# A graph layer on one core: messages turned by the scaled W_o1, 48 tiles prepared alone, fetches a chunk ahead, 36 blocks summed after the last message

## The chip, the core and the metric

The kernel runs on one core of a Trainium2 chip. The core has five engines with queues of their own: PE (matrix products; its weight loads are listed as PEld), DVE or VectorE, ACT or ScalarE, POOL or GpSimd, and SP, which only issues transfers. Sixteen DMA engines serve all queues. The metric is the device time of one execution in microseconds (us); the time before is the median of three runs.

## The reference, cut to what matters

There are 12500 nodes with 128 features, and 400000 edges with 20 features each. `dst` is sorted, `src` is not; messages are gathered by `dst` and summed by `src`.

```python
def smu(x, alpha=0.01, mu=2.5):
    return ((1 + alpha) * x + (1 - alpha) * x * erf(mu * (1 - alpha) * x)) / 2

hx = maximum(layernorm(x), 0.0)
h = hx @ W_in2f.T
Wij = smu(f_ij @ W_f1.T + b_f1) @ W_f2.T + b_f2
Wij = Wij * rcut_ij[:, None]
x_ij = h[dst] * Wij
agg = segment_sum(x_ij, src, num_segments=12500)
out = x + smu(agg @ W_o1.T + b_o1) @ W_o2.T + b_o2
```

`smu` is a Gelu plus a small linear part; the kernel computes it as `Gelu(ZS * v) + LIN * v` and puts the remaining factor into the next matrix.

## The kernel before, in words

**Units of work.** A tile is 128 edges (3125 of them), a group 4 tiles (782), a super 8 tiles (two groups). A bin is 128 nodes (98 of them, the last with 84). The edges are worked in 9 passes (`PARTS`: 59, 59, 59, 59, 48, 37, 27, 27 and 16 supers). In a pass every message is written to a buffer in HBM, ordered by its source bin, with 129 numbers per row (128 values and its row in the bin). While the next pass prepares its messages, the buffer of the pass before is read back and summed into `agg`, in "blocks": one block is 128 rows of one bin, summed with a one-hot matrix in one product. A bin of pass k has Q[k] blocks (6 in the first four passes, then 5, 4, 3, 3, 2). A fetch brings 12 row-columns at most, so 4 bins of 3 blocks in the last pass but one; there are four such row buffers (`rw`), and `AHEAD = 4`.

**A group.** PE multiplies the edge features (L551, `hide`), ACT takes the Gelu (L559), DVE adds the linear part (L567, `smooth`), PE multiplies by W_f2 (L604, `weigh`). For the gather, h in three bf16 parts lies in HBM; SP loads the 42 rows that a group's sorted targets can reach (L451, at a row number read from `base_i`), DVE makes a one-hot matrix from the targets (L460), and PE multiplies (L585). ACT copies that out of PSUM (L593, `take`), DVE multiplies the two (L614, `mix`), PE transposes the four tiles (L624, `turn`), and ACT scales each by its edge weight into the message tile `ms` (L634, `send`). DVE puts the row in the bin beside it (L631), and POOL writes one tile at a time with an indirect transfer (L637). Where it writes is counted in between: a running count per bin on DVE (L485, `bins`), products that rank the tile's edges (L499 to L502, `count`), a maximum (L529, `read`) and the address (L538, `number`).

**The order.** PE, DVE, ACT and SP run in the order in which the program is written; POOL's instructions are placed by a planner, by readiness. In the loop over groups an iteration writes: `turn(g)`, `send(g)`, `step()`, `number`, `weigh`, `gather`, `take` for g+1, half of the blocks due (`parts`), `mix(g+1)`, `step()`, `hide`, `bend`, `count`, `smooth` for g+2, `bins(g+3)`, `read(g+2)`, the other half of the blocks, `step()`. So DVE's small cast of group g stands in its queue behind the work of the iteration before.

**The opening.** Tiles 0 to 23 (`FEW`) have their targets in the first 128 rows of h, which are computed first and kept on the chip (`h_first`); their gather is three products (L583) and needs no window. Meanwhile 14 opening steps (rows 128 to 511 of h, targets and bins of the first chunk of 512 tiles) are taken two per `step()`. Later steps of pass 0 (the other six chunks of indices: `head_of`, whose `fetched` issues the index loads and whose `based` is the first to use them; statistics and rows of h) are spread over the rest of that pass.

**The end.** After the last group, the last pass's buffer is fetched and summed. Every four bins form an output unit: a product with W_o1 (L250), a Gelu (L251), the linear part on DVE (L255), four products with W_o2 (L260), the sum with x and bias (L264) and the store. x is loaded four units ahead on ACT's queue (L240), and POOL adds the bias to it (L246). Each x tile is asked for when the unit four before it has been stored.

## Time and profile before

| what | us |
|---|---|
| three runs: median (lowest to highest) | 4151.15 (4150.53 to 4153.11) |
| the profiled execution: time | 4134.27 |
| its span | 4132.4 |
| first scatter, last scatter (L637 starts) | 19.15, 4023.79 |
| busy: PE, DVE, ACT, POOL | 3500.0, 3498.8, 1854.6, 3048.9 |
| ACT waiting to write a message for a free buffer (L634) | 474.5 |
| DVE waiting for fetched rows (L679), 11 times | 147.2 |
| mean granted PE clock | 0.959 |

A timeline line reads: start (us), duration (us), engine, line of the kernel, operation, written tile <- read tiles, partitions x elements, and in brackets the idle time of that engine before it and what ended it. A group line ends with busy us, mean ns of one, and idle us before. A windows line gives a stretch and its length, then busy us and instruction counts of PE, PEld, DVE, ACT and POOL, and then PE's granted clock, the share of the 16 DMA engines, and GB/s.

### The profile page before, as it was taken

The page shows a single profiled execution, that of the slowest core. Times are in us where ns is not written, and L with a number is a line of the kernel's source. Part 1 is how long each engine was busy: PE and PEld are TensorE (multiplying, and loading weights), DVE is VectorE, ACT ScalarE, POOL GpSimd, SP SyncE. Part 2 cuts the span into 40 slices and gives each one's busy share as a digit, 9 for nine tenths or more (in the row PEclk, how much of TensorE's full clock was granted, in tenths as well). Part 3 has the DMA queues.
Part 4 walks back from the last instruction along what each step waited for, and adds up shares of the span by engine and source line. Part 5 has one row for each costly group of instructions (what it writes and reads, how often), then busy time and mean ns, then how long its engine had stood idle before and what let it go on. Part 6 is the DMA issues. An engine that isn't in the chain of part 4 may idle for free. (4 is left out here: it accounts for less than half of the span.)

```text
span 4132.4 us, 67973 instructions
## 1 busy us (share of the span) xinstructions
PE 3500.0 (85%) x18032; PEld 2218.3 (54%) x18032; DVE 3498.8 (85%) x8551; ACT 1854.6 (45%) x4810; POOL 3048.9 (74%) x3173
## 2 busy tenths in 40 slices
PE   6767886988887888869888879998799889898888
PEld 2334444555554555545555546665466556565567
DVE  6898886988887988869888869998799889898887
ACT  3446553544444444435444434444344444444431
POOL 4777777777777777777777777777777777777772
PEclk8999998999998999989999989999899999999999
DMA  4875665766656766647666647776588689787568
GB/s 144 234 198 174 189 186 176 211 193 193 196 156 200 211 197 190 199 140 214 214 189 194 201 149 209 215 212 199 173 233 230 176 244 248 211 234 219 170 184 240
DMA packets 564967, 820.60 MB, mean 199 GB/s; under 512 B 178779, under 2 KB 379234, under 8 KB 564444
## 3 DMA queue, kind: packets, MB, share of 16 engines
q1 hardware_dynamic: 450650, 602.06, 51.1%
q0 software_dynamic: 100320, 207.40, 15.2%
q10 hardware_dynamic: 13602, 6.73, 0.6%
q8 instruction: 143, 2.34, 0.3%
q14 instruction: 252, 2.06, 0.2%
HBM read 442.51 MB, written 373.37 MB: 197 GB/s over the span
## 5 line engine op out<-in xcount | busy, mean ns | idle before, releaser
L637 POOL DMA_INDIRECT buf<-ms,ix x3125 | 3008.6, 963 | 1006.6 <-issue 424.8
L634 ACT ACTIVATE ms<-pt,w_sb 128x128 f32<-128x128 f32 x3125 | 890.9, 368 | 1442.2 <-PE pt L624 848.6
L692 PEld LDWEIGHTS pg<-se,rw 128*128 128x128 f32 x8036 | 1060.6, 193 | 267.0 <-issue 225.1
L692 PE MATMUL pg<-se,rw 128*128 128x128 f32 x8036 | 1154.2, 281 | 8.5 <-DVE se L679 8.5
L485 DVE SCALAR_TENSOR_TENSOR so<-irow_ps,hi_f,so 128x98 f16<-128x98 f32 x3116 | 989.8, 318 | 82.6
L624 PE MATMUL pt<-ident,mt 128*128 128x128 f32 x3125 | 507.2, 286 | 524.7 <-DVE mt L614 522.0
L604 PE MATMUL pw<-sm,w_f 128*128 128x512 f32 x1564 | 902.9, 660 | 42.6 <-DVE sm L567 40.7
L551 PE MATMUL pu<-f,w_f 128*128 128x512 f32 x1564 | 824.5, 610 | 0.0
L559 ACT ACTIVATE ge<-pu 128x512 f32<-128x512 f32 x782 | 469.1, 600 | 555.4 <-PE pu L551 540.2
L679 DVE TENSOR_TENSOR se<-irow_ps,rw 128x1536 f32<-128x1536 f32 (+1 forms) x345 | 587.8, 1704 | 148.4 <-DMA rw<-buf 147.2
L614 DVE SCALAR_TENSOR_TENSOR mt<-pw,b,hg 128x512 f32<-128x512 f32 x782 | 583.3, 746 | 145.8 <-ACT hg L593 133.9
L624 PEld LDWEIGHTS pt<-ident,mt 128*128 128x128 f32 x3125 | 348.2, 143 | 624.5 <-DVE mt L614 618.2
L567 DVE SCALAR_TENSOR_TENSOR sm<-pu,ge 128x512 f32<-128x512 f32 x782 | 534.9, 684 | 151.6 <-ACT ge L559 147.1
L593 ACT ACTIVATE hg<-ph 128x512 f32<-128x512 f32 x782 | 469.1, 600 | 170.0 <-PE ph L585 99.6
L529 DVE TENSOR_REDUCE sl<-pc 128x4 f32<-128x392 f32 x782 | 434.7, 556 | 0.0
L604 PEld LDWEIGHTS pw<-sm,w_f 128*128 128x128 f32 x1564 | 240.3, 194 | 164.2 <-DVE sm L567 136.4
L585 PE MATMUL ph<-oh,hw 126*128 126x512 bf16 x776 | 306.4, 395 | 0.0
L551 PEld LDWEIGHTS pu<-f,w_f 128*128 128x128 f32 x1564 | 258.7, 199 | 59.5 <-issue 52.0
L499 PE MATMUL pc<-so,tri 128*128 128x392 f16 x782 | 260.6, 333 | 1.9 <-DVE so L485 1.1
L501 PE MATMUL pc<-so,rest_h 128*128 128x294 f16 x781 | 227.4, 291 | 0.0
L501 PEld LDWEIGHTS <-rest_h 128*128 128x128 f16 x781 | 77.1, 99 | 272.4 <-issue 272.3
L460 DVE TENSOR_SCALAR oh<-rbc,prow 128x1024 bf16<-128x1024 bf16 x388 | 192.8, 497 | 1.5 <-DMA rbc<-rel_dram 1.5
(151 smaller groups left out, 1357.5 us busy)
## 6 DMA issues: line engine op xcount, KB each, us to landing
rw<-buf SPq DMA_DIRECT2D x292, 774.0 KB
rbc<-rel_dram SPq DMA_DIRECT2D x389, 256.0 KB
buf<-zero SPq DMA_DIRECT2D x243, 387.0 KB
buf<-ms,ix POOLq DMA_INDIRECT x3125
buf<-zero SPq DMA_DIRECT2D x193, 258.0 KB
rw<-buf SPq DMA_DIRECT2D x49, 645.0 KB
f<-in_f_t SPq DMA_DIRECT2D x390, 80.0 KB
hw<-h_dram SPq DMA_DIRECT2D x776, 31.5 KB
```

What stands on the lines that cost most here:

```text
L485: nc.vector.scalar_tensor_tensor(so[:, j], irow_ps[:, :NB], hi_f[:, t + j:t + j + 1], so[:, j - 1] if j else before, op0=ALU.is_equal, op1 ...
L551: nc.tensor.matmul(pu[:, :n], w_f1, loaded[g // PER][0][:, o:o + n], start=True, stop=True)
L559: nc.scalar.activation(ge[:, :n], units_of[g][:, :n], AF.Gelu, scale=ZS)
L567: nc.vector.scalar_tensor_tensor(sm[:, :n], units_of.pop(g)[:, :n], LIN, hidden[g][:, :n], op0=ALU.mult, op1=ALU.add)
L593: nc.scalar.activation(hg[:, :n], rows_of[g][:, :n], AF.Copy)
L604: nc.tensor.matmul(pw[:, :n], w_f2, hidden.pop(g)[:, :n], start=True, stop=True)
L614: nc.vector.scalar_tensor_tensor(mt[:, :n], pws.pop(g)[:, :n], b2, rows_of.pop(g)[:, :n], op0=ALU.add, op1=ALU.mult)
L624: nc.tensor.transpose(pt[:, j, :], mt[:, j * P:(j + 1) * P], ident)
L634: nc.scalar.activation(ms[:, j, 0:P], pt[:, j], AF.Copy, scale=w_sb[:, t + j:t + j + 1])
L637: i = nc.gpsimd.indirect_dma_start(out=bufs[k][:, :], out_offset=bass.IndirectOffsetOnAxis(ap=ix[:, j:j + 1], axis=0), in_=ms[:, j, :], in ...
L679: nc.vector.tensor_tensor(se[:, :m], irow_ps.unsqueeze(1).to_broadcast([P, m, P]), rows_in[c][:, :m, P:P + 1].to_broadcast([P, m, P]), op= ...
L692: nc.tensor.matmul(pgs[0][:, g, :], rows_in[c][:, o, 0:P], sel[c][:, o, :], start=(q == 0), stop=(q == Q[k] - 1))
```

## The change

It has ten parts, all in one diff. (1) W_o1, scaled by LIN, takes the place of the identity in `turn`, so that a message reaches the buffer already multiplied by W_o1; the sums are then `LIN * agg @ W_o1.T`, and the output units lose their product. Gelu's scale becomes ZS / LIN, and the linear part is a plain sum. (2) In the output units Gelu reads `agg` itself, and the sum is done on POOL (`between`); the four PSUM tiles rotate for W_o2's products. (3) The row-in-bin numbers are copied by ACT instead of DVE. (4) The scaling in the layer norm goes from DVE to ACT, with a new tile `down` for minus mean times the reciprocal. (5) Bin and row in the bin come from float arithmetic (`whole_bins`: rounding by a large constant) instead of an integer shift and mask: five operations in place of four. (6) 48 tiles instead of 24 are prepared with `h_first`. (7) One opening step per `step()` instead of two. (8) `fetched` of chunk c+1 stands ahead of the steps of chunk c. (9) In the last pass 36 of the 294 blocks are left out of the loop and summed after the last group, with the last pass's first fetches written ahead of them. (10) w_o1 is loaded at the start, on ACT's queue, instead of by SP later.

```diff
@@ -34,6 +34,7 @@
 ROW = P + 1
 BIG = 2047.0
 ZP = 128
+ROUND = 12582912.0
 
 
 @with_exitstack
@@ -184,6 +185,7 @@
     x_sb = agg.rearrange("p (b d) -> p b d", d=D)
     mv = const.tile([P, NB, 2], F32, name="mv")
     rstd = const.tile([P, NB], F32, name="rstd")
+    down = const.tile([P, NB], F32, name="down")
 
     def stats(pool, b):
         st = pool.tile([P, 6], F32, name="st")
@@ -193,13 +195,14 @@
     def deviations(a, b):
         nc.scalar.activation(rstd[:, a:b], mv[:, a:b, 1], AF.Sqrt, bias=eps)
         nc.vector.reciprocal(rstd[:, a:b], rstd[:, a:b])
+        nc.vector.scalar_tensor_tensor(down[:, a:b], mv[:, a:b, 0], -1.0, rstd[:, a:b], op0=ALU.mult, op1=ALU.mult)
 
     def rows_of_h(b, n, xn, xt, left, hs, psum):
 
         def normed():
             for j in range(n):
-                nc.vector.tensor_scalar(xn[:, j], x_sb[:, b + j, :], mv[:, b + j, 0:1], rstd[:, b + j:b + j + 1],
-                                        op0=ALU.subtract, op1=ALU.mult)
+                nc.scalar.activation(xn[:, j], x_sb[:, b + j, :], AF.Identity, scale=rstd[:, b + j:b + j + 1],
+                                     bias=down[:, b + j:b + j + 1])
 
         def turned():
             pt = kept[0] = psum("pt")
@@ -248,11 +251,11 @@
     def half(unit, po, ge):
         w = width(unit)
         nc.tensor.matmul(po[:, :w], w_o1, agg[:, unit[0] * P:unit[0] * P + w], start=True, stop=True)
-        nc.scalar.activation(ge[:, :w], po[:, :w], AF.Gelu, scale=ZS, bias=bz)
+        nc.scalar.activation(ge[:, :w], po[:, :w], AF.Gelu, scale=ZS / LIN, bias=bz)
 
     def bent(unit, po, ge, sm):
         w = width(unit)
-        nc.vector.scalar_tensor_tensor(sm[:, :w], po[:, :w], LIN, ge[:, :w], op0=ALU.mult, op1=ALU.add)
+        nc.vector.tensor_add(sm[:, :w], po[:, :w], ge[:, :w])
 
     def rest(unit, sm, py):
         b, n, rows = unit
@@ -286,7 +289,7 @@
         def fill(i, engine):
             engine.memset(fbufs[i], 1.0)
 
-        FEW = 3 * SUP
+        FEW = 6 * SUP
 
         def parts_tile():
             return edge.tile([P, GRP, 3, D], BF, name="hs")
@@ -295,6 +298,13 @@
 
         def bank(name):
             return ps2.tile([P, GRP, P], F32, name="pg")
+
+        def whole_bins(to, sf, si):
+
+            nc.vector.tensor_copy(sf, si)
+            nc.vector.tensor_scalar(to, sf, 1.0 / P, -(P - 1) / (2.0 * P), op0=ALU.mult, op1=ALU.add)
+            nc.vector.tensor_scalar(to, to, ROUND, None, op0=ALU.add)
+            nc.vector.tensor_scalar(to, to, -ROUND, None, op0=ALU.add)
 
         def head_of(c):
 
@@ -303,6 +313,7 @@
             s0, m = a // GRP, (n + GRP - 1) // GRP
             rw = rowp.tile([P, ROWS, ROW], F32, name="rw").rearrange("p q r -> p (q r)")
             di, si, rel = rw[:, 0:n].bitcast(I32), rw[:, CH:CH + n].bitcast(I32), rw[:, 2 * CH:2 * CH + n]
+            sf = rw[:, 0:n]
             rb = parts_tile()[:, :, 0, :]
             z = 0 if c else FEW
             base_f = edge.tile([1, CH // GRP], F32, name="base_f")
@@ -357,12 +368,11 @@
                 nc.vector.tensor_scalar(base_i[:, :early], base_f[:, :early], float(HEAD * P - WIN), None, op0=ALU.min)
 
             def binned():
-                nc.vector.tensor_scalar(di[:, z:], si[:, z:], 7, None, op0=ALU.arith_shift_right)
-                nc.vector.tensor_copy(hi_f[:, a + z:a + n], di[:, z:])
+                whole_bins(hi_f[:, a + z:a + n], sf[:, z:], si[:, z:])
 
             def placed():
-                nc.vector.tensor_scalar(di[:, z:], si[:, z:], P - 1, None, op0=ALU.bitwise_and)
-                nc.vector.tensor_copy(lo_b[:, a + z:a + n], di[:, z:])
+                nc.vector.scalar_tensor_tensor(lo_b[:, a + z:a + n], hi_f[:, a + z:a + n], -float(P), sf[:, z:],
+                                               op0=ALU.mult, op1=ALU.add)
 
             return dict(fetched=fetched, based=based, spread=spread, lowered=lowered, turned=turned, written=written,
                         limits=limits, bounded=bounded, binned=binned, placed=placed)
@@ -372,6 +382,7 @@
         ds = edge.tile([P, FEW], I32, name="ds", bufs=1)
         ss = edge.tile([P, FEW], I32, name="ss", bufs=1)
         dsf = edge.tile([P, FEW], F32, name="dsf", bufs=1)
+        ssf = edge.tile([P, FEW], F32, name="ssf", bufs=1)
         h_first = const.tile([P, 1, 3, D], BF, name="h_first")
         nc.sync.dma_start(ds, dst_col[:, 0:FEW])
         nc.scalar.dma_start(x_sb[:, 0:1, :], bin_rows(x, 0, 1))
@@ -382,6 +393,7 @@
         nc.gpsimd.dma_start(w_f1[0:R, :], w_f1_t)
         nc.gpsimd.dma_start(w_f1[R:R + 1, :], b_f1)
         nc.sync.dma_start(fbufs[0][0:R, :], f_t[:, 0:SUP * P])
+        nc.scalar.dma_start(w_o1, w_o1_t)
         nc.scalar.dma_start(x_sb[:, 1:HEAD, :], bin_rows(x, 1, HEAD - 1))
         nc.gpsimd.dma_start(w_f2, w_f2_t)
         nc.gpsimd.dma_start(b2, b_f2.rearrange("o p -> p o"))
@@ -402,7 +414,6 @@
         def late_loads():
 
             nc.sync.dma_start(w_sb[:, CH:NT], w_col[:, CH:NT])
-            nc.sync.dma_start(w_o1, w_o1_t)
 
         def later_loads():
             nc.sync.dma_start(w_o2, w_o2_t)
@@ -426,7 +437,7 @@
             if s > 0:
                 nc.sync.dma_start(fb[0:R, :n], f_t[:, e0:e0 + n])
             loaded[s] = (fb,)
-            if s > 3:
+            if s > 2:
                 targets(s)
 
         def targets(s):
@@ -621,14 +632,14 @@
             pt = ps1.tile([P, GRP, P], F32, name="pt")
             mt = mixed.pop(g)
             for j in range(n):
-                nc.tensor.transpose(pt[:, j, :], mt[:, j * P:(j + 1) * P], ident)
+                nc.tensor.matmul(pt[:, j, :], mt[:, j * P:(j + 1) * P], w_o1, start=True, stop=True)
             mixed[g] = pt
 
         def send(g):
 
             t, n = groups[g]
             ms = msg.tile([P, GRP, ROW], F32, name="ms")
-            nc.vector.tensor_copy(ms[:, :n, P], lo_b[:, t:t + n])
+            nc.scalar.activation(ms[:, :n, P], lo_b[:, t:t + n], AF.Copy)
             pt = mixed.pop(g)
             for j in range(n):
                 nc.scalar.activation(ms[:, j, 0:P], pt[:, j], AF.Copy, scale=w_sb[:, t + j:t + j + 1])
@@ -717,11 +728,10 @@
                 done += 1
 
         WAIT = 4
+        LEFT = 36
         def few_bins():
-            nc.vector.tensor_scalar(ds, ss, 7, None, op0=ALU.arith_shift_right)
-            nc.vector.tensor_copy(hi_f[:, 0:FEW], ds)
-            nc.vector.tensor_scalar(ds, ss, P - 1, None, op0=ALU.bitwise_and)
-            nc.vector.tensor_copy(lo_b[:, 0:FEW], ds)
+            whole_bins(hi_f[:, 0:FEW], ssf, ss)
+            nc.vector.scalar_tensor_tensor(lo_b[:, 0:FEW], hi_f[:, 0:FEW], -float(P), ssf, op0=ALU.mult, op1=ALU.add)
 
         def other_starts():
             m = tiles_of(0)
@@ -762,6 +772,7 @@
         loaded[0] = (fbufs[0], None, h_first.rearrange("p b k d -> p (b k d)"))
         hide(0)
         nc.vector.tensor_scalar(w_f2, w_f2, GC, None, op0=ALU.mult)
+        nc.vector.tensor_scalar(w_o1, w_o1, LIN, None, op0=ALU.mult)
         for b in range(1, HEAD):
             stats(edge, b)
         deviations(1, HEAD)
@@ -838,12 +849,16 @@
         loads = [lambda a=a, n=n: old_piece(HEAD + a, n) for a, n in chunks(NB - HEAD, PIECE)]
         single = [lambda b=b: stats(edge, b) for b in range(HEAD, NB)]
         steps = [one["placed"], loads.pop(0), one["limits"]]
+        heads_of = [named(lambda c=c: head_of(c),
+                          ("fetched", "based", "spread", "lowered", "turned", "written", "binned", "placed", "limits"))
+                    for c in range(1, NC)]
+        steps.append(heads_of[0].pop(0))
         for c in range(1, NC):
-            mine = named(lambda c=c: head_of(c),
-                         ("fetched", "based", "spread", "lowered", "turned", "written", "binned", "placed", "limits"))
             if loads:
                 steps.append(loads.pop(0))
-            for f in mine:
+            if c + 1 < NC:
+                steps.append(heads_of[c].pop(0))
+            for f in heads_of[c - 1]:
                 steps.append(f)
                 if c > 1:
                     steps.append(single.pop(0))
@@ -863,9 +878,7 @@
 
             nonlocal taken_steps, slot
             if opening:
-                for _ in range(2):
-                    if opening:
-                        opening.pop(0)()
+                opening.pop(0)()
                 return
             slot += 1
             while taken_steps < COUNT and taken_steps * 3 * (eps_of[0][1] * PER - 15) < slot * COUNT:
@@ -877,9 +890,8 @@
             k = epoch[s]
             g0, ng = eps_of[k][0] * PER, min(eps_of[k][1] * PER, NG - eps_of[k][0] * PER)
             i = g - g0
-            if g == 2:
-                assert len(opening) == 2
-                targets(3)
+            if g == (FEW // SUP - 3) * PER:
+                assert not opening
             if g % PER == 0:
                 load(s + 3)
             if i == 0:
@@ -904,8 +916,9 @@
                 choose(k - 1, 0)
             lo = hi = 0
             if k and i >= WAIT:
-                lo = len(work) * (i - WAIT) // (ng - WAIT)
-                hi = len(work) * (i + 1 - WAIT) // (ng - WAIT)
+                upto = len(work) - (LEFT if k == EPOCHS - 1 else 0)
+                lo = upto * (i - WAIT) // (ng - WAIT)
+                hi = upto * (i + 1 - WAIT) // (ng - WAIT)
             if g:
                 turn(g)
                 send(g)
@@ -930,6 +943,7 @@
             assert k == 0 or taken_steps == COUNT
         k = EPOCHS - 1
         begin(k)
+        parts(k - 1, len(work))
         choose(k, order_of[k][0])
 
 
@@ -950,24 +964,26 @@
 
         def other(i, names):
             turns[i] += 1
-            return names[turns[i] % 2]
+            return names[turns[i] % len(names)]
+
+        def part_of(unit):
+            return agg[:, unit[0] * P:unit[0] * P + width(unit)]
 
         def first_half():
             unit = ready.pop(0)
-            po = ps1.tile([P, GRP * P], F32, name=other(0, ("pu", "ph")))
             ge = edge.tile([P, GRP * P], F32, name="ge")
-            half(unit, po, ge)
-            opened.append((unit, po, ge))
+            nc.scalar.activation(ge[:, :width(unit)], part_of(unit), AF.Gelu, scale=ZS / LIN, bias=bz)
+            opened.append((unit, ge))
 
         def between():
-            unit, po, ge = opened.pop(0)
+            unit, ge = opened.pop(0)
             sm = edge.tile([P, GRP * P], F32, name="sm")
-            bent(unit, po, ge, sm)
+            nc.gpsimd.tensor_add(sm[:, :width(unit)], part_of(unit), ge[:, :width(unit)])
             smoothed.append((unit, sm))
 
         def second_half():
             unit, sm = smoothed.pop(0)
-            py = ps1.tile([P, GRP, P], F32, name=other(1, ("pw", "pt")))
+            py = ps1.tile([P, GRP, P], F32, name=other(0, ("pu", "ph", "pw", "pt")))
             rest(unit, sm, py)
             summed.append((unit, py))
 
```

## The prediction

> **What bounds the kernel now.** I read the page first. PE and DVE are both busy 85% of the span, GpSimd 74%, and the chain of waits is spread over twenty lines, so no total names the limit. I then read GpSimd's own timeline in the middle of the run.
>
> ```profile
> PE 3500.0 (85%) x18032; PEld 2218.3 (54%) x18032; DVE 3498.8 (85%) x8551; ACT 1854.6 (45%) x4810; POOL 3048.9 (74%) x3173
> L637 POOL DMA_INDIRECT buf<-ms,ix x3125 | 3008.6, 963 | 1006.6 <-issue 424.8
> ```
> ```profile
> 1012.72 0.96 POOL L637 DMA_INDIRECT buf<-ms,ix  x1 [0.30 <-DMA buf<-ms,ix]
> 1013.99 0.96 POOL L637 DMA_INDIRECT buf<-ms,ix  x1 [0.30 <-issue]
> 1015.25 0.95 POOL L637 DMA_INDIRECT buf<-ms,ix  x1 [0.30 <-ACT ms L634]
> ```
>
> The scatter of one tile takes 0.96 us, and the next one starts 0.30 us later whatever releaser is named: 1.263 us from start to start, 5.05 us for a group of four tiles. 3124 such steps make 3945.6 us. The first scatter starts at 19.15 us and the last at 4023.79, so 4004.6 us lie between them: GpSimd's issue is the bound, and all that can be won there is 59 us of holes. What is left is 19 us ahead and 108.6 us behind. Where are the holes?
>
> ```profile
> 23.06 0.95 POOL L637 DMA_INDIRECT buf<-ms,ix  x1 [0.30 <-issue]
> 31.05 0.95 POOL L637 DMA_INDIRECT buf<-ms,ix  x1 [7.03 <-issue]
> 34.83 0.96 POOL L637 DMA_INDIRECT buf<-ms,ix  x1 [0.30 <-issue]
> 40.91 0.96 POOL L637 DMA_INDIRECT buf<-ms,ix  x1 [5.12 <-ACT ge L559]
> 56.88 0.96 POOL L637 DMA_INDIRECT buf<-ms,ix  x1 [0.30 <-issue]
> 68.78 0.96 POOL L637 DMA_INDIRECT buf<-ms,ix  x1 [10.94 <-issue]
> ```
>
> In the first ten groups, the holes beyond the 1.263 add up to 31.4 us (6.7, 4.8, 2.0, 10.6, 3.1, 2.9, 1.4 ahead of groups 1, 2, 3, 5, 6, 9, 10). Groups 19 to 98 have some 5 us, the last pass (groups 750 to 781) 9 us; the rest are single scatters that are a little slow. The second place is the end, where GpSimd has no scatter left:
>
> ```profile
> 4060.83 1.13 PE L260 MATMUL pw<-w_o,sm 128*128 128x128 f32 x8
> 4061.80 1.02 PE L250 MATMUL ph<-agg,w_o 128*128 128x512 f32 x2
> 4062.66 1.95 PE L692 MATMUL pg<-se,rw 128*128 128x128 f32 x16
> 4064.48 1.13 PE L260 MATMUL pt<-w_o,sm 128*128 128x128 f32 x8
> 4065.44 1.02 PE L250 MATMUL pu<-agg,w_o 128*128 128x512 f32 x2
> ```
> ```profile
> 4030.00:4040.00 10.00, 8.09 (x49) 7.83 (x49) 6.26 (x8) 0.70 (x2) 0.00 (x0) 0.64 0.81 263
> 4040.00:4070.00 30.00, 30.00 (x212) 25.44 (x212) 24.45 (x31) 5.50 (x8) 8.97 (x8) 1.00 0.95 279
> 4070.00:4100.00 30.00, 30.00 (x217) 25.91 (x216) 25.06 (x30) 6.12 (x9) 10.40 (x9) 1.00 0.99 290
> 4100.00:4120.00 20.00, 20.00 (x147) 17.42 (x146) 14.42 (x21) 3.50 (x6) 8.03 (x7) 1.00 0.62 183
> ```
>
> PE runs without a gap at 3.64 us per output unit of four bins: 1.82 for the sums, 0.96 for W_o2, 0.86 for W_o1 (starts to starts). But the last three columns (clock, DMA share, GB/s) say that the 16 DMA engines are 95 to 99% busy as well.
>
> **The change, part by part.**
>
> *Start.* VectorE's chain to the first message gets a reciprocal's follower (0.17, as L195's 0.16) and the scaling of W_o1 (0.22, as L764), the four integer operations become five, and the turn is longer (next part): +0.9 us. L721 stands there with 4.85 us and ends at 8.98, its twin L723 takes 0.18; GpSimd's fills run from 4.61 to 8.94. I take it that the new first arithmetic operation waits for the fills too. The bound on the other side is that the delay belongs to the integer shift and goes with it: -4.7. The Trainium skill (Advanced Engine Details and Errata, Mode Summary under VectorE Performance Modes) says that VectorE's second SBUF port is GpSimd's too, and that two-port instructions and GpSimd block each other; by that the wait stays, and the two ends of the rows agree with it in time.
>
> *Turn.* 3125 transposes (one instruction each, 109 ns start to start) become products with W_o1 (two instructions, 112 ns as L692): 0.44 us per group become 0.90, +0.46 on PE, of which 0.05 to 0.15 hides behind the next product's wait for VectorE (weigh waits for sm). The bound below is nothing, where VectorE sets the pace. It only counts where the groups are prepared more slowly than 5.05 us. I read that pace from the turns' starts after each pass boundary: 4.65 us in passes 1 to 3, 4.82 in pass 5, 5.02 in pass 6, 4.84 in pass 7, 5.43 in the last. PE idles ahead of the turn (the waits, by window) 70.5 us in 115 groups of pass 1, 13.0 us in 61 groups of pass 5 (0.21 each), 12.7 us in 47 groups of pass 6 (0.27). So pass 5 becomes 5.03 at most, still below 5.05; pass 6 some 5.17, 50 groups x 0.12 = 6 us, of which 3 are covered by the lead that messages have after a boundary (4 us). Together **+3**, with ends 0 and +72 (no idle time takes anything: the slower rival).
>
> *The bin numbers of a message go from VectorE to ScalarE.* The trace has no such operation on ScalarE; the 128x1 square root takes 0.28, a 128x128 copy advances by 0.285, VectorE's own cast by 0.11. I take 0.2. ScalarE has 2.34 us of work in 5.05 per group and runs it while PE turns, so it costs nothing; without that cover 0.2 x 782. VectorE gains 0.11 per group. It waits for a free message buffer, as the first copy behind it does already (474.5 us of waits by ScalarE), so nothing new is queued behind it. What counts: group 1's message was done at 28.1, but VectorE's cast stood behind four other operations until 30.1, and the scatter waited for it.
>
> *Opening.* 48 tiles from the first 128 rows, one step per call, 14 calls for 14 steps, the rows' scaling on ScalarE, chunk 1's indices fetched a chunk ahead (the window loads of groups 6 to 11 go from SP, 2.9 us a pair; their gather costs two more matmuls, 0.43). Hole by hole: group 1 loses 2.6 (cast) and 0.85 (three scalings on VectorE), gets 0.45: 6.7 to 3.7. Group 2: PE stood 3.5 us for L330, which now lies two calls ahead of the transposes: 4.8 to 1. Group 3: 2.0 to 0.5. Group 5: VectorE stood 7.57 us for chunk 1's indices.
>
> ```profile
> 59.20 0.26 DVE L317 COPY base_i<-rw 1x128 int32<-1x128 int32 x1 [7.57 <-DMA rw<-in_dst_col]
> ```
>
> Two more steps now lie between fetch and use, about a group or 5 us: 10.6 to 2.5. Group 6: 3.1 to 2. Group 9 (chunk 2's indices, 4.46 us of waiting): 2.9 to 0. Group 10: 1.4 to 0.5. Sum 31.4 to 10: **-21**. Ends: -28 and -8. Later in pass 0 VectorE loses 98 scalings (0.28 each) and gets one more operation per chunk (0.45 x 7): **-2** of the 5 us.
>
> *Last pass.* 36 of 294 blocks leave: over 28 groups 2.6 matmuls each, 0.29 on PE, about 0.24 on VectorE; the turn adds 0.46, the cast takes 0.11. The pace stays at about 5.4, but scatters no longer wait for VectorE's cast (group 780: message done 4016.4, scatter 4018.7): **-3**. The 36 blocks (72 x 0.112 = 8.1 us on PE) fall into the 10.5 us between the last turn (4018.44) and the first selection of the last sums (4028.93), in which PE sat 8.5 us: no cost. Without that cover the rest beyond 10.5 us counts. They hold all four row buffers, so SP's fetches wait for them as well as for the last scatters; only stores stand behind.
>
> *Output.* W_o1 leaves: 0.86 of 3.64 us, PE's bound becomes 2.78. Gelu reads agg; the sum goes to GpSimd (two adds of 1.27, as L246: 2.54 per unit). By PE alone 24 x 0.86 = -21. By the DMA row 0.97 x 3.64 = 3.53 us of transfers per unit: -3. Between them: the shares times their stretches from 4026 on add up to 87 us, so transfers could end at 4113, some 19 us before the end, of which about 5 remain for the last unit's chain: -14 at most. I take **-11**, the clock (0.64 around 4035, since PE sat idle) among it.
>
> Sum: 0.9 - 21 - 2 + 3 - 3 - 11 = **-33 us**. The profiled execution took 4134.27 us (span 4132.4, 1.9 around it), 16.9 below the median of the three runs, 4151.15. I set the difference against the median: **4118 us**.
>
> **Rivals.**
> (a) *Transfers hold the output* at 3.53 or more: -22 in all, 4129. For it: the share of 0.99. Against: it falls to 0.62 while PE still works.
> (b) *GpSimd's queue holds the output.* If the bias add of a later unit, which waits for its rows of x, stands ahead of the sum, a loop closes over two units: x issue to bias 4.9 us (5.79 us idle before one), two adds 2.54, W_o2 1.13, store 0.69 and hops: 9.3 us, 4.65 per unit early, about 4.2 on average: +13 instead of -11, 4142. Against it: over three units, which is the order by readiness, it gives 3.1. The Trainium skill (GPSIMD Engine Reference, Engine selection) advises against adds on GpSimd, some twice VectorE's time; the rows have 1.27 against 0.68.
> (c) *The opening keeps half its holes*, since 14 calls at one step last until group 4 with GpSimd starved: -10 instead of -21, 4129; with the queue (b) together, 4150.
> (d) *PE becomes the bound of the middle, slower.* If the 0.46 adds to every group's pace, it passes 5.05 already in pass 1 (5.11): 3 each in passes 1 to 3, then 5.30 x 92 groups, 5.28 x 70, 5.48 x 50, 5.30 x 50 less 3 us lead each: 9 + 20 + 13 + 18 + 9 = 69, last pass +3. In all +39, 4190. It decides once 0.24 of the 0.46 is not absorbed in pass 5. For it: PE is 95.8% busy from 3000 to 3200. Against: much of that is modelled ends, and the idle times above.
> (e) *No effect*: the opening's waits only move and the output stays: near 4147.
>
> **How the numbers follow.** Forecast 0.53, (a) 0.12, (b) 0.09, (c) 0.09, (d) 0.12, (e) 0.05. The likeliest's own range is 4103 to 4134. Leaving out the upper part of (d) and the best of the forecast gives 4094 to 4156. A measurement tells 0.2% (8.3 us) from no change: below 4142.8 lie nearly all of the forecast, (a), (c), half of (b): 0.76; within, the rest of (b), (e): 0.10; above, (d) and mixtures: 0.14.
>
> **What would show it.** Right: scatters 1.263 us apart from group 12 on, holes of about 10 us ahead of it, L317 waiting under 3 us, output units 3.1 to 3.4 us apart, last scatter near 4002. Wrong: holes all through passes 4 to 7 with PE back to back (d); GpSimd waiting for x with a sum behind it (b); a first scatter at 15 us (the shift's own delay).

## The result, and the profile after

| | before | changed |
|---|---|---|
| median of four runs, us (lowest to highest) | 4150.84 (4149.83 to 4153.11) | 4107.88 (4107.29 to 4114.07) |
| ratio, 95% interval | | 0.9897 (0.9885 to 0.9909) |
| the profiled execution, us | 4134.27 | 4108.47 |
| first scatter, last scatter | 19.15, 4023.79 | 19.90, 4001.50 |
| holes between scatters: groups 0 to 11 | 32.1 | 7.8 |
| groups 12 to 117 (rest of pass 0) | 8.2 | 4.6 |
| passes 1 to 7 | 9.1 | 15.7 |
| last pass | 9.6 | 7.8 |
| from the last scatter to the end of the span | 108.6 | 105.1 |

The changed kernel is 43 us faster by the medians and 25.8 us by the two profiled executions. Holes are counted as in the prediction: the distance between two starts of scatters, less 1.263 us for every scatter. The step that ends at the first scatter of group 12 is counted with groups 0 to 11, and so at each later boundary. Both columns add up: 3945.6 us of steps plus 59.0 of holes before, 36.0 after.

The page of the changed kernel, its first part and the group of the scatters:

```profile
PE 3668.0 (89%) x21117; PEld 2553.0 (62%) x21117; DVE 3445.1 (84%) x7657; ACT 1948.2 (47%) x5690; POOL 3081.7 (75%) x3199
L648 POOL DMA_INDIRECT buf<-ms,ix x3125 | 3011.3, 964 | 981.5 <-issue 384.1
```

PE has gained 168 us of work and 3085 instructions and is busy 89% of the span; the kernel is faster all the same, because GpSimd's idle time ahead of its scatters fell from 1006.6 to 981.5. Its timeline in the opening, the three scatters of the first twelve groups that waited longer than 0.6 us, and that of group 5:

```profile
27.43 0.96 POOL L648 DMA_INDIRECT buf<-ms,ix  x1 [2.67 <-ACT ms L645]
...
47.80 0.96 POOL L648 DMA_INDIRECT buf<-ms,ix  x1 [0.30 <-ACT ms L645]
...
66.23 0.96 POOL L648 DMA_INDIRECT buf<-ms,ix  x1 [3.18 <-ACT ms L645]
...
83.32 0.96 POOL L648 DMA_INDIRECT buf<-ms,ix  x1 [1.75 <-ACT ms L645]
```

Group 5, which had waited 10.94, starts its scatter at 47.80 with the usual 0.30. Three holes of more than a microsecond are left, ahead of groups 1, 8 and 11. The start, on VectorE (first lines) and GpSimd (the fills):

```profile
3.89 5.10 DVE L304 CAST ssf<-ss 128x48 f32<-128x48 int32 x1
9.02 0.19 DVE L305 TENSOR_SCALAR hi_f<-ssf 128x48 f32<-128x48 f32 x1
...
4.61 0.97 POOL L290 MEMSET f<- 128x1024 f32 x1
...
7.97 0.97 POOL L290 MEMSET f<- 128x1024 f32 x1
```

The new first arithmetic operation takes the old one's place: it stands until the last fill is over. At the other end, the last sums:

```profile
3998.39 0.49 PE L635 MATMUL pt<-w_o,mt 128*128 128x128 f32 x2 [0.92 <-DVE mt L625]
3998.72 10.49 PE L703 MATMUL pg<-se,rw 128*128 128x128 f32 x92
4009.58 0.69 DVE L690 TENSOR_TENSOR se<-irow_ps,rw 128x512 f32<-128x512 f32 x1
```

After the last turn PE has 92 instructions, 46 blocks, to do, and VectorE makes the first selection of the last sums only at 4009.58, 8.1 us after the last scatter (a selection is the one-hot matrix of a fetch, L690). Before, it came at 4028.93, 5.1 us after.

### The profile page after: what moved, and what is told of

Same layout as the page of the kernel before. It is cut to its first block, busy times and chain, and to the rows that moved or that the text cites. A ratio compares the mean times of both kernels' runs of the same rounds, so it can differ in the third digit from the quotient of the medians.

```text
span 4106.6 us, 74086 instructions
## 1 busy us (share of the span) xinstructions
PE 3668.0 (89%) x21117; PEld 2553.0 (62%) x21117; DVE 3445.1 (84%) x7657; ACT 1948.2 (47%) x5690; POOL 3081.7 (75%) x3199
## 3 DMA queue, kind: packets, MB, share of 16 engines
q1 hardware_dynamic: 449760, 601.83, 54.7%
q0 software_dynamic: 100320, 207.40, 15.9%
## 4 chain that ended last, share of the span: by engine, by line
PE 38%; DVE 28%; DMA 19%; ACT 6%; issue 5%; POOL 2%; DVEq 0%; SPq 0%; ACTq 0%; POOLq 0%
DMA buf<-ms,ix 17%; PE pt L635 11%; PE pg L703 8%; DVE se L690 8%; PE pw L615 8%; PE pu L562 7%; DVE mt L625 5%; DVE so L496 4%; DVE sm L578 3%; DVE sl L540 3%; ACT ms L645 2%; ACT ge L570 2%; POOL buf L648 2%; PE ph L596 2%; DVE agg L716 1%
## 5 line engine op out<-in xcount | busy, mean ns | idle before, releaser
L648 POOL DMA_INDIRECT buf<-ms,ix x3125 | 3011.3, 964 | 981.5 <-issue 384.1
L635 PE MATMUL pt<-w_o,mt 128*128 128x128 f32 x6250 | 883.7, 285 | 386.0 <-DVE mt L625 382.4
L635 PEld LDWEIGHTS pt<-w_o,mt 128*128 128x128 f32 x6250 | 768.5, 194 | 472.9 <-DVE mt L625 468.9
L615 PE MATMUL pw<-sm,w_f 128*128 128x512 f32 x1564 | 823.0, 609 | 10.7 <-DVE sm L578 8.8
L562 PE MATMUL pu<-f,w_f 128*128 128x512 f32 x1564 | 807.3, 598 | 0.0
L690 DVE TENSOR_TENSOR se<-irow_ps,rw 128x1536 f32<-128x1536 f32 (+1 forms) x345 | 588.0, 1704 | 114.0 <-DMA rw<-buf 109.1
L604 ACT ACTIVATE hg<-ph 128x512 f32<-128x512 f32 x782 | 468.5, 599 | 59.7 <-PE ph L596 42.9
L642 ACT ACTIVATE ms<-lo_b 128x4 f32<-128x4 bf16 x782 | 160.1, 205 | 339.8 <-DMA buf<-ms,ix 339.4
L596 PE MATMUL ph<-oh,hw 126*128 126x512 bf16 x770 | 297.0, 386 | 0.0
```

The lines of the kernel that those rows point to most:

```text
L562: nc.tensor.matmul(pu[:, :n], w_f1, loaded[g // PER][0][:, o:o + n], start=True, stop=True)
L615: nc.tensor.matmul(pw[:, :n], w_f2, hidden.pop(g)[:, :n], start=True, stop=True)
L635: nc.tensor.matmul(pt[:, j, :], mt[:, j * P:(j + 1) * P], w_o1, start=True, stop=True)
L648: i = nc.gpsimd.indirect_dma_start(out=bufs[k][:, :], out_offset=bass.IndirectOffsetOnAxis(ap=ix[:, j:j + 1], axis=0), in_=ms[:, j, :], in ...
L690: nc.vector.tensor_tensor(se[:, :m], irow_ps.unsqueeze(1).to_broadcast([P, m, P]), rows_in[c][:, :m, P:P + 1].to_broadcast([P, m, P]), op= ...
```

## The experiments

The runs were made on four chips, in the groups of the table; the kernel before ran beside each group. On three of these chips every kernel, the unchanged one too, takes about a quarter longer; what they can tell is said with each reading. From the last scatter to the end, kernels with the same code there differ by some 4 us from trace to trace (105.1 to 109.4 on the chips of 4100 us, 103.5 to 107.1 on the others). Columns: median; ratio to the kernel before on the same chip; holes of groups 0 to 11, 12 to 117, passes 1 to 7, last pass; and the tail after the last scatter, all in us.

| kernel | median | ratio (95%) | 0-11 | 12-117 | 1-7 | last | tail |
|---|---|---|---|---|---|---|---|
| before, again (before: 5237.7) | 5229.1 | 1.0012 (0.9976 to 1.0048) | 35.5 | 150.2 | 934.8 | 46.5 | 112.1 |
| turn_plain | 4981.0 | 0.9538 (0.9489 to 0.9586) | 22.2 | 119.3 | 736.8 | 38.4 | 114.8 |
| open_24 | 5031.2 | 0.9646 (0.9599 to 0.9692) | 23.7 | 126.8 | 761.3 | 47.0 | 107.1 |
| left_none | 5021.3 | 0.9618 (0.9571 to 0.9666) | 16.8 | 125.7 | 791.4 | 48.7 | 102.2 |
| changed, again (before: 5268.8) | 5091.4 | 0.9662 (0.9604 to 0.9720) | 16.5 | 134.7 | 815.3 | 49.3 | 103.5 |
| sum_dve | 5084.7 | 0.9642 (0.9586 to 0.9699) | 14.4 | 129.2 | 821.9 | 49.6 | 102.1 |
| fetch_late (before: 4140.6) | 4126.6 | 0.9966 (0.9953 to 0.9978) | 17.8 | 10.4 | 16.7 | 7.2 | 109.4 |
| cast_dve | 4120.2 | 0.9947 (0.9930 to 0.9963) | 13.0 | 7.4 | 18.7 | 9.4 | 106.7 |
| fills_act | 4107.1 | 0.9918 (0.9901 to 0.9934) | 8.4 | 5.0 | 18.0 | 6.6 | 105.4 |
| best_sum | 4102.2 | 0.9910 (0.9893 to 0.9926) | 8.4 | 6.0 | 15.9 | 10.1 | 97.9 |
| turn_plain, again (before: 5273.6) | 5036.1 | 0.9575 (0.9515 to 0.9635) | 14.8 | 125.8 | 754.6 | 54.7 | 115.5 |
| open_24, again | 5097.8 | 0.9676 (0.9617 to 0.9734) | 25.4 | 131.7 | 825.4 | 54.0 | 106.7 |

### The kernel before, once more

> The kernel before, unchanged, with a trace of another execution. Its first traced execution took 4134.3 us, the median of its runs is 4150.8; the changed kernel's traced execution (4108.5) agrees with its median (4107.9). So the two traces differ by 25.8 us and the medians by 43.0, and 17 us of the gain lie where no trace shows them yet. Theory A (the old trace was one lucky execution): a new trace takes about 4150 us and shows the 16 us as more holes between scatters, in the opening or in the passes. Theory B (tracing itself changes this kernel): the new trace takes 4134 again, with 59 us of holes, and the timed runs 4150.

Neither theory was tested: the chip was another one, and the kernel took 5229 us. The timeline of that execution in pass 3, first PE, then ScalarE:

```profile
1995.37 0.38 PE L585 MATMUL ph<-oh,hw 126*128 126x512 bf16 x1
1996.26 1.02 PE L551 MATMUL pu<-f,w_f 128*128 128x512 f32 x2
...
2000.62 0.60 ACT L593 ACTIVATE hg<-ph 128x512 f32<-128x512 f32 x1 [3.83 <-remote]
2006.33 0.60 ACT L559 ACTIVATE ge<-pu 128x512 f32<-128x512 f32 x1 [5.11 <-remote]
```

Single operations last as long as on the first chip (scatter 0.96, copy 0.60, Gelu 0.60). But the copy that reads `ph` starts 4.9 us after that product has ended, and the Gelu that reads `pu` 9.1 us after, and the profile finds no other work that they waited for ("remote" is what it says when it knows no releaser). The semaphore events that the trace has for these two waits come 0.02 and 0.03 us ahead of the starts, so the hand-over itself is late there. The traces of these three chips hold only about a third of the semaphore events of the others (36 thousand here, 95 thousand in the trace of before), so a releaser that they name is worth less. The bound of the middle is no longer GpSimd's issue: holes are spread over all passes, 1.5 us in every group (934.8 in 632).

### The whole change, once more, and the sum on VectorE

```diff
-            nc.gpsimd.tensor_add(sm[:, :width(unit)], part_of(unit), ge[:, :width(unit)])
+            nc.vector.tensor_add(sm[:, :width(unit)], part_of(unit), ge[:, :width(unit)])
```

> The changed kernel, unchanged, beside the kernel before on whatever chip this call gets. In the call before this one every kernel took 20 to 26% longer, with the same durations of single instructions but pauses of 2 to 9 us in which ScalarE starts nothing though its inputs have long been there. If that belongs to that chip: here about 4108, a ratio to before of 0.990, and a trace with 36 us of holes. If it belongs to the kernels' day-to-day spread: above 4900 again, with a ratio near 0.96, as the variants had.

> The changed kernel with the sum of an output unit on VectorE (0.68 us) instead of GpSimd (1.27). In the changed trace PE waits for that sum in 15 of 25 units, 0.3 to 1.8 us each, 13 us in all, and units are 3.30 us apart. If GpSimd's two adds per unit set the pace: units fall to 2.8 to 3.0, time 7 to 12 us less (4096 to 4101). If the transfers set it (share 1.01 of the 16 DMA engines from 4040 to 4080): units stay at 3.2 to 3.3, time within 3 us of the changed kernel (4105 to 4108), and PE waits for the sum as long, since the sum waits for a buffer that a store has to free.

The unchanged change gives 0.966 there, 177 us. The quarter is thus not the kernel's usual spread, since the third chip below is back at 4140; and the change is worth more where hand-overs are late. The tail reads nearly as on the first chip (103.5 against 105.1); the opening's holes are twice as large (16.5 against 7.8). With the sum on VectorE the two ratios cannot be told apart, and the tail is only 1.3 us shorter, less than it differs by between traces. But inside the tail the effect can be seen: from the first product with W_o2 to the last it takes 74.5 us instead of 79.9, and PE waits 8.2 us for the sums instead of 13.2. Neither expectation holds as it stands: units are 3.1 us apart on average instead of 3.3, and PE's wait shrinks. The rest of the tail took the gain back in this execution: the first product comes 1.7 us later behind the last scatter, and the end is 2.4 longer.

The expectation's 3.30 us per unit was a miscount: from the product of one unit at 4024.70 to that of the nineteenth after it at 4090.65 there are 65.95 us, 3.47 per unit.

### Messages turned by the identity

```diff
-                nc.tensor.matmul(pt[:, j, :], mt[:, j * P:(j + 1) * P], w_o1, start=True, stop=True)
+                nc.tensor.transpose(pt[:, j, :], mt[:, j * P:(j + 1) * P], ident)
 ...
-            nc.scalar.activation(ge[:, :width(unit)], part_of(unit), AF.Gelu, scale=ZS / LIN, bias=bz)
+            half(unit, po, ge)
 ...
-            nc.gpsimd.tensor_add(sm[:, :width(unit)], part_of(unit), ge[:, :width(unit)])
+            bent(unit, po, ge, sm)
```

> The changed kernel with parts 1 and 2 undone: messages turned by the identity, a product with W_o1, its Gelu and the sum on VectorE in every output unit. From the traces: output units 3.64 us apart instead of 3.30, 24 x 0.34 = +8 us; passes 1 to 7 get back 6.6 us of holes, the last pass some; together +1 to +3 us, 4109 to 4111. Rival (GpSimd's adds cost the output more than W_o1 did): not above 4104. Rival (the turn's second instruction costs nothing in the middle): +8, 4116.

> The changed kernel with parts 1 and 2 undone, once more, beside a kernel before that takes about 4140 to 4150 us. From the runs so far: the tail after the last scatter grows from 105 to 113 to 115 us (114.8 on the slow chip, units 3.65 us apart), and the holes of passes 1 to 7 shrink from 15.7 to about 9 us: net +2 to +4 us on the changed kernel. Rival (PE is near the bound of the middle, as 78 us on the slow chip say): the holes shrink by less than 3 us here, since there are only 16, and the net is +6 to +9.

Both were run beside a kernel before of more than 5200 us, so the net on the first chip's pace was not measured. What can be read there is the tail: 114.8 and 115.5 with W_o1 in the output, 102.1 to 107.1 without it on such chips, 8 to 13 us, and units 3.65 us apart. In the middle the second instruction of the turn costs 25 to 71 us of holes in 632 groups there, against kernels with the product on the same chip (736.8 against 761.3 and 791.4, 754.6 against 825.4), 0.04 to 0.11 per group. On the chips of 4100 us, five traces with the product have 15.7 to 18.7 us of holes in passes 1 to 7, and the one without it 9.1. Where the kernel before takes more than 5200, the kernel without the product is the fastest of its group, so parts 1 and 2 lose there. On the chips of 4100 us it is 7 to 10 us more holes against 7.5 us less for the output (below); which way the net goes there was not shown.

### Which part filled the opening

```diff
 ...
         for c in range(1, NC):
+            mine = named(lambda c=c: head_of(c),
+                         ("fetched", "based", "spread", "lowered", "turned", "written", "binned", "placed", "limits"))
             if loads:
                 steps.append(loads.pop(0))
-            if c + 1 < NC:
-                steps.append(heads_of[c].pop(0))
-            for f in heads_of[c - 1]:
+            for f in mine:
```

> The changed kernel with part 8 undone: a chunk's indices are fetched one step before they are used. The prediction put 11 of the opening's 21 us on this part (group 5 from 10.6 to 2.5, group 9 from 2.9 to 0). If so: VectorE's copy of chunk 1's indices waits 6 to 8 us again, the holes of the first 12 groups grow by 8 to 11 us, and the ratio to before rises by 0.002. Rival (one step per call spreads the steps enough): holes grow by less than 4 us.

As predicted: VectorE's copy of chunk 1's indices waits again, and the scatter of group 7 with it.

```profile
62.76 0.26 DVE L328 COPY base_i<-rw 1x128 int32<-1x128 int32 x1 [8.24 <-DMA rw<-in_dst_col]
...
68.08 0.95 POOL L648 DMA_INDIRECT buf<-ms,ix  x1 [10.49 <-ACT ms L645]
```

The holes of the first twelve groups grow by 10.0 us, of which 4.0 stand ahead of the first scatter of group 12 (there VectorE waits for the indices of chunk 2); those of the rest of pass 0 grow by 5.8. VectorE waits 16.3 us at four of its copies of indices, and at none with the fetch ahead. The other 4.3 us of its 20 lie in the tail, whose code is the same; its units were 3.60 apart in this execution and 3.47 in the other, so this much is put down to the spread of the tail. The ratio rose by 0.007 where 0.002 was expected, since the rest of pass 0 and that spread were not in it.

```diff
-            nc.scalar.activation(ms[:, :n, P], lo_b[:, t:t + n], AF.Copy)
+            nc.vector.tensor_copy(ms[:, :n, P], lo_b[:, t:t + n])
```

> The changed kernel with part 3 undone: the row numbers are cast on VectorE, behind the work of the iteration before. Prediction: 2.6 us in the opening (group 1) and part of 3 us in the last pass, nothing elsewhere: holes +3 to +6 us in all, ratio to before 0.991 where the changed kernel has 0.990. On a chip where hand-overs between engines are late (the calls so far: 5091 for the changed kernel, 0.966 of before), a rival: the cast is one more hand-over before every scatter, and its move is worth 50 us or more there: ratio above 0.975. Against: below 0.970.

More than predicted: 13 us behind fills_act, which ran beside it with the cast on ScalarE (and an earlier start, worth 1.4); and its last scatter starts at 4014.05, 12.5 us after that of the changed kernel's trace. Group 1 shows how; first this kernel, with the cast on VectorE, then the changed one:

```profile
26.80 1.14 ACT L645 ACTIVATE ms<-pt,w_sb 128x128 f32<-128x128 f32 x4 [1.11 <-PE pt L635]
28.49 0.16 DVE L642 CAST ms<-lo_b 128x4 f32<-128x4 bf16 x1
29.40 0.96 POOL L648 DMA_INDIRECT buf<-ms,ix  x1 [4.62 <-ACT hg L604]
```
```profile
25.58 0.20 ACT L642 ACTIVATE ms<-lo_b 128x4 f32<-128x4 bf16 x1
26.79 1.14 ACT L645 ACTIVATE ms<-pt,w_sb 128x128 f32<-128x128 f32 x4 [1.01 <-PE pt L635]
27.43 0.96 POOL L648 DMA_INDIRECT buf<-ms,ix  x1 [2.67 <-ACT ms L645]
```

The messages are written at the same time in both. With the cast on ScalarE, ahead of them, the first scatter may start when the first tile is written; on VectorE the cast for the whole group comes at 28.49 and holds even the first tile back, by 1.97 us. The holes grow in every stage: 5.2 us more in the first twelve groups than in the changed kernel's trace, 2.8 in the rest of pass 0, 3.0 in passes 1 to 7 (5.1 more in pass 6 alone, less elsewhere), 1.6 in the last, 12.6 together; against fills_act, on the same chip, 10.5. The expectation had 3 to 6. Its rival, 50 us or more where hand-overs are late, was not tested: this chip is one of 4100 us.

```diff
-        FEW = 6 * SUP
+        FEW = 3 * SUP
 ...
             if opening:
-                opening.pop(0)()
+                for _ in range(2):
+                    if opening:
+                        opening.pop(0)()
```

> The changed kernel with 24 tiles prepared alone and two opening steps per call (parts 6 and 7 undone). If the opening's gain of 24 us is theirs: holes of 20 to 26 us in the first 12 groups instead of 7.8, time 4120 to 4126. Rival (the gain belongs to the cast on ScalarE and to the fetch a chunk ahead): holes of 10 to 14 us, 4110 to 4114. If the 17 us that the traces do not show lie in the opening: 4135 to 4143.

> The changed kernel with parts 6 and 7 undone, once more, beside a kernel before that takes about 4140 to 4150 us. The fetch a chunk ahead was worth 10 us of the opening's holes and the cast on ScalarE 5; 24 went. If the rest is parts 6 and 7 (48 tiles, one step per call): holes of the first 12 groups 16 to 18 us instead of 7.8, last scatter 8 to 10 us later. Rival (the parts overlap, and any two of them do): holes below 12 us.

The holes are 23.7 and 25.4 where traces of the changed opening on such chips have 14.4 to 16.8 and, in two kernels that turn by the identity, 14.8 and 22.2. So 48 tiles and one step per call are worth some 8 us on these chips, with one trace that blurs it. 10.0 + 5.2 + 8 make 23 of the opening's 24. That is agreement, not proof: the 8 come from chips of another pace, what the parts save can overlap, and parts 4, 5 and 10 were never undone alone.

### The blocks left over

```diff
-        LEFT = 36
+        LEFT = 0
```

> The changed kernel with no blocks left over after the last group (LEFT = 0). In the trace of the changed kernel the first selection of the last sums starts 8.1 us after the last scatter (5.1 before), so the 36 blocks cost 3 us there; in the last pass they free 0.29 us of PE per group over 28 groups, 8 us, of which the scatters see what is not lead. If the part pays: holes of the last pass 7.8 grow to 14 to 16 us, the wait at the end shrinks by 3, time 4110 to 4114. Rival (it only moves work behind the last scatter): the holes grow by less than 3 us, 4105 to 4108.

The rival's reading holds on that chip, whose times are not the ones expected: the holes of the last pass stay (48.7, and 47.0 in open_24 on the same chip). What the blocks cost behind the last scatter can be read: without them VectorE's first selection of the last sums comes 5.6 us after it and waits for its fetch; in three traces with 36 blocks on such chips (open_24 and its repeat, the changed kernel) it comes 9.2 after it, and VectorE has not been idle before it.

```profile
4953.92 0.69 DVE L690 TENSOR_TENSOR se<-irow_ps,rw 128x512 f32<-128x512 f32 x1 [3.70 <-DMA rw<-buf]
```

The last scatter of left_none started at 4948.29. On that chip the last pass has 1.2 to 1.5 us of holes per group in every kernel, so what the part frees on PE may be lost in it; on a chip of 4100 us it was tried only together with two other parts, below.

### What holds VectorE at the start, and a faster version

```diff
-        fill(1, nc.gpsimd)
-        fill(2, nc.gpsimd)
-        fill(3, nc.gpsimd)
+        def copy_ones(i):
+            nc.scalar.activation(fbufs[i].rearrange("p (a b) -> p a b", b=P),
+                                 onesb.unsqueeze(1).to_broadcast([P, SUP, P]), AF.Copy)
 ...
         take(0)
+        for s in (1, 2):
+            copy_ones(s)
+            load(s)
```

> The changed kernel with the three fills of feature buffers (0.97 us each on GpSimd between 4.6 and 8.9 us) done by ScalarE after 16 us. In the changed trace VectorE's cast L304 stands from 3.89 to 8.99, as long as GpSimd's memsets run. If GpSimd's memsets hold VectorE: the cast ends by 6 to 7 us and the first scatter starts at 17 to 18 us instead of 19.9, time 2 to 3 us less. Rival (the cast of int32 numbers itself, or its load, takes that long): the cast still ends near 9 and the first scatter stays at 19.9 to 21.

GpSimd's fills hold VectorE. The same cast in fills_act, from the timelines of VectorE and (last line) GpSimd:

```profile
3.89 0.43 DVE L308 CAST ssf<-ss 128x48 f32<-128x48 int32 x1
4.35 0.36 DVE L309 TENSOR_SCALAR hi_f<-ssf 128x48 f32<-128x48 f32 x1
4.75 0.69 DVE L310 TENSOR_SCALAR hi_f<-hi_f 128x48 f32<-128x48 f32 x1
...
4.61 0.78 POOL L406 MEMSET zero<- 128x774 f32 x1
```

5.10 us become 0.43, and the first scatter starts at 16.45 instead of 19.90. Of these 3.45 us the last scatter, 4000.06 instead of 4001.50, has kept 1.4: group 1's hole is 0.7 longer, and passes 1 to 7 have 2.3 more, within what traces of like kernels differ by.

The last kernel takes these fills, the sum on VectorE and `LEFT = 18`:

> The changed kernel with ScalarE's fills, the sum of the output units on VectorE and 18 blocks left over instead of 36. If the start gives 2 to 3, the sum 1 to 3 (the tail was 102.1 us after the last scatter with the sum on VectorE, 103.5 with it on GpSimd, on one chip) and the shorter rest 1 to 2: 5 to 7 us less than the changed kernel, 4101 to 4103, or 0.001 to 0.002 off its ratio to before. Rival: the last sums wait for the same transfers either way, and nothing but the start is left: 2 to 3 us.

4102.2 us, 4.9 less than fills_act on the same chip and the lowest time here (ratio 0.9910; that chip's kernel before took 4140.6; single runs of the two kernels overlap). The tail is 7.5 us shorter (97.9): units are 3.24 us apart instead of 3.47, and the last sums start 6.2 us after the last scatter (4002.15) instead of 8.1:

```profile
4008.39 0.69 DVE L691 TENSOR_TENSOR se<-irow_ps,rw 128x512 f32<-128x512 f32 x1 [2.88 <-DMA rw<-buf]
```

With 18 blocks this selection waits for its fetch again, so these blocks do not hold it up. The last pass gives back 3.5 us of holes, since the other 18 blocks are in it again. So the number of blocks left over moves time between the last pass and the tail. The gain is the closer units': from the first product with W_o2 to the last it takes 74.9 us instead of 80.6, 5.7 less, and the sum on VectorE alone took 5.4 off this stretch in sum_dve.

## Why the prediction was right, point by point

The forecast was 4118 us in a range of 4094 to 4156; 4107.88 lies inside, on the good side. Its mechanism, holes filled in the opening at little cost in the middle, is what happened: the last scatter starts at 4001.50, where 4002 was named, with 7.8 us of holes up to group 12, where 10 were named. Some terms were mis-sized, one step failed, and the base was off by more than any of them. That the total came within 10 us is luck in part: the sum was 7 us too favourable by the traces, and the base left out a difference of 17 (last point below).

**Start**, +0.9: +0.75. That the new first operation waits for GpSimd's fills was the right choice between the two ends, and fills_act showed the cause.

**Opening**, -21: -24.3. The fetch a chunk ahead was put at 11 and measured 10.0. The hole ahead of group 8 (2.87 beyond the step) was not foreseen. No engine waits for the transfer of chunk 1's indices any more; but PE waits for VectorE's copies of them, which stand in VectorE's queue:

```profile
57.87 0.22 DVE L329 CAST base_f<-base_i 1x128 f32<-1x128 int32 x1
58.14 1.12 PE L337 MATMUL pg<-base_f,ones 1*128 1x512 f32 x2 [2.40 <-DVE base_f L329]
```

Of the rivals on the opening, (c) fell: a quarter of the holes stayed, not half. (Its time together with (b) should have read 4153 by the prediction's own terms, not 4150.)

**The cast**, put at no cost and a gain of 2.6 in group 1 and a part of the last pass's 3: 12.6 us in the traces (10.5 against fills_act). The cover on ScalarE was real, and its copy took the 0.20 us assumed (L642). What was mis-sized is how often a scatter waited for VectorE's queue: I had looked for it only where the trace of before showed large holes.

**Turn in the middle**, +3: passes 1 to 7 went from 9.1 to 15.7, +6.6. The sum had put its cost into pass 6, but the holes of pass 6 stayed (2.9 before, 3.0 after); passes 1 to 5 got 4.1 more and pass 7 2.5, most of it in steps that are under 0.3 us late. In pass 6 the cast on ScalarE works the other way: with it back on VectorE, the same pass has 8.0. So the term was put into the wrong pass, and came out twice as large. The lines of PE's waits, before and after:

```profile
PE pt L624 <- DVE mt L614: 522.0, 428, 22.1
```
```profile
PE pt L635 <- DVE mt L625: 382.4, 363, 22.3
```

PE's wait for `mt` shrank by 140 us, 0.18 per group: that much of the 0.46 was absorbed there. The distance of the turns, over groups 8 to 50 of each pass, rose by 0.15 us per group in pass 5 (4.79 to 4.94), by 0.12 in pass 6 (5.07 to 5.19) and by 0.15 in pass 7 (4.93 to 5.08), not by 0.46. So rival (d), PE as the bound of the middle, fell on this chip. Where hand-overs are late the same product costs 25 to 71 us; that PE is the reason there was not shown (in the kernel before it is busy 74% of the span there, 85% on the first chip).

**Rest of pass 0**, -2: -3.5. **Last pass**, -3: -1.8.

**The 36 blocks**, at no cost: +3.0 us. This is the step that failed. I laid them into the 10.5 us between the last turn and the first selection of before, of which PE sat 8.5:

```profile
4018.44 0.33 PE L624 MATMUL pt<-ident,mt 128*128 128x128 f32 x1 [0.34 <-DVE ms L631]
...
4028.93 0.69 DVE L679 TENSOR_TENSOR se<-irow_ps,rw 128x512 f32<-128x512 f32 x1 [7.25 <-DMA rw<-buf]
```

But 5.35 us of that gap were the lead of the last message over its scatter (turn at 4018.44, scatter at 4023.79). With ScalarE's cast the lead is 3.1 (3998.39, 4001.50), so the gap is 2.2 shorter, and the 46 blocks that lie in it take 10.5 us. VectorE then selects 8.1 us after the last scatter and has waited for no fetch; before, it had waited 7.25 us for one. Three runs bear this out: with the cast back on VectorE and the same 36 blocks (cast_dve) the lead is 5.4 (4008.61, 4014.05) and the selection comes 6.5 after the last scatter, and with 18 blocks or none it waits for its fetch, 6.2 and 5.6 after. The step of the prediction that was wrong is thus the cover: it took the lead of before as part of the gap, and another part of the change took 2.2 us of that lead away.

**Output**, -11: from the first selection to the last addition 89.5 us instead of 97.0, -7.5; the end behind it is 1.0 longer. Units are 3.47 us apart where I had 3.1 to 3.4. The sign that I had named for rival (b) is there. The timelines of ScalarE, GpSimd and PE around one unit of the changed kernel:

```profile
4045.99 0.72 ACT L975 ACTIVATE ge<-agg,bz 128x512 f32<-128x512 f32 x1 [3.27 <-DVE ms L267]
...
4047.84 1.27 POOL L249 TENSOR_TENSOR hg<-hg,bo 128x512 f32<-128x512 f32 x1 [2.50 <-DMA hg<-in_x]
4049.06 1.26 POOL L981 TENSOR_TENSOR sm<-agg,ge 128x512 f32<-128x512 f32 x1
...
4050.38 1.16 PE L263 MATMUL pt<-w_o,sm 128*128 128x128 f32 x8 [1.82 <-POOL sm L981]
```

The Gelu is done at 4046.71, but the sum stands on GpSimd behind the bias addition of a later unit, which waits for x until 4047.84; PE then waits 1.82 us for the sum. In 15 of 25 units this adds up to 12.5 us of PE. So (b) is there in part: units come 3.47 us apart, not the 4.2 that it gave. Rival (a) said that transfers would hold units at 3.53 us or more, and fell with best_sum, whose units are 3.24 apart. What may limit them next can be seen in the windows of the changed kernel and, below, of best_sum (the third busy time is VectorE's, the last three columns are PE's clock, the DMA share and GB/s):

```profile
4040.00:4060.00 20.00, 16.83 (x143) 16.06 (x143) 13.90 (x16) 4.33 (x6) 14.89 (x12) 1.00 1.01 312
4060.00:4080.00 20.00, 17.23 (x144) 16.28 (x144) 14.46 (x17) 4.22 (x6) 14.03 (x12) 1.00 1.02 308
```
```profile
4040.00:4060.00 20.00, 17.81 (x151) 16.90 (x150) 18.58 (x23) 4.78 (x7) 6.78 (x7) 1.00 1.08 326
4060.00:4080.00 20.00, 17.67 (x149) 16.72 (x148) 18.58 (x23) 4.56 (x7) 9.31 (x8) 1.00 0.97 293
```

With the sum on VectorE, PE waits 7.2 us for it instead of 12.5, and units come no closer than 3.24, well above PE's 2.68 (1.79 for the sums and 0.89 for W_o2 from start to start where nothing waits). VectorE is then busy 18.58 of 20 us, where it was at 13.9 to 14.5, and the DMA share lies between 0.97 and 1.08. By these rows VectorE is the nearest bound of best_sum's output, with the transfers close by; no run separates the two.

**The base.** By the traces the terms add up to -25.8, not -33. I set the difference against the median, which lay 16.9 us above before's traced execution, as if that distance were the kernel's and would stay. It did not: the changed kernel's traced execution and its median agree within 0.6. So 17 of the 43 us lie in executions of the kernel before that no trace shows. The traced execution of before is not among the four of its median and lies 15.6 us below the lowest of them, while these four differ by 3.3; whether it ran on the same chip the record does not say. If not, the 17 us are a difference of chips: on another chip the kernel before took 4140.6, and on three others 5229 to 5274; on the one of these where the changed kernel itself ran, it gained 177. That late hand-overs, which the changed kernel has fewer of per scatter, are behind the 17 us is another explanation. Neither was tested; it stays open.

## What to carry to other kernels

Where one engine issues at a fixed pace, count its holes stage by stage: the totals of this profile moved the wrong way (PE busier by 168 us) while the kernel got faster. A small operation that completes a message belongs on the engine that writes the message, ahead of it: on another engine's queue it cost 12.6 us, most of it in holes of under 2 us each. And work laid into a gap at the end fits only into the part of the gap that the other parts of the change leave there.

## What the runs showed of the hardware

**VectorE behind GpSimd's fills.** The cast of 128x48 numbers took 5.10 us beside five memsets and 0.43 without three of them; and L310 above, started at 4.75, took 0.69 instead of 0.19 (L306 of the changed kernel) and ended at 5.44, just after the memset that the timeline has from 4.61 to 5.39. The Trainium skill (SBUF — State Buffer, SBUF: two separate sides) says that the port pair which the two share is held for a whole instruction and the other engine is blocked fully. The 0.69 agrees. The 5.10 goes further: the cast starts 0.7 us ahead of the first memset by the profile, and it does not get in between them. Why, the trace does not show.

**Chips differ by a quarter.** The kernel before had medians of 4141 and 4151 us on two chips and of 5229 to 5274 on three, with equal durations of single operations on VectorE, ScalarE and GpSimd. On the slow chip of the lines above, signals arrive 4.9 and 9.1 us late; PE is busy 74% of the span instead of 85%, its mean granted clock is 0.873 instead of 0.959, and its product L604 takes 754 ns on average instead of 660. What delays the signals was not found.
